# Retention's output in three float32r products, the norms' scaling on VectorE, and two tiles for a bias

## The chip, the cores and the metric

The kernel runs on one core of a Trainium2 chip, in one launch. The metric is device time in microseconds (us) of that core, from three runs of the kernel. An execution taken by the hardware profiler gives the span, which is the time from the first to the last instruction, and the busy time of each engine: TensorE (PE, with PEld for its weight loads), VectorE (DVE), ScalarE (ACT), GpSimd (POOL) and SyncE (SP), whose queue issues the DMAs.

## The reference

The reference is a stack of four layers on x of shape 8 x 1024 x 256, in float32, each of the form x + layer(layernorm(x)):

```python
x = x + _L0_attn_a_ref(_layernorm(x), ...)   # retention, 4 heads; itself returns its input + out
x = x + _L0_ffn_ref(_layernorm(x), ...)      # f
x = x + _L0_attn_b_ref(_layernorm(x), ...)   # softmax attention, 16 heads of 16, relative bias
x = x + _L0_ffn_ref(_layernorm(x), ...)      # g, the same weights as f
```

In the retention layer the input is normed once more with a weight and a bias (`ln_w`, `ln_b`), projected to q, k, v and a gate g, and after the heads it ends in

```python
o = o * lax.rsqrt((o ** 2).mean(-1, keepdims=True) + EPS) * g_norm_w
o = o * (g * jax.nn.sigmoid(g))
out = o.reshape(B, T, 2 * D) @ Wo        # (T x 512) @ (512 x 256) per batch
return x + out
```

The attention layer has scores q k / 4 plus a bias that depends on the distance of query and key alone (32 buckets), a softmax over 1024 keys, and projections with biases.

## The kernel before

**How it is written.** `layer_kernel` does not issue instructions itself. Each call on an engine (`act`, `dve`, `pool`, `sp`, `pe`) is recorded by `Plan.record` with an estimated cost (`Plan.estimate` for ACT, DVE and POOL, the `cost` argument in `mm` for PE) and a target time. Then `Plan.issue` plays all operations on five queues, picks for each engine the ready operation with the earliest target, and emits it (`emit`, line 609, which is why every row of the profile has this line). What results is a fixed order for each engine. `RULES` and `TURNS` steer the choice on PE: each stretch of 20 planned microseconds has one of 16 rules, one hexadecimal digit of `TURNS` each. On the chip every engine runs its list in that order and waits where data are late, so a change of any estimate, or of `TURNS`, moves instructions everywhere.

**The work.** The batches b = 0 to 7 go through retention, the first feed-forward (`ffn_front`), the projections of the attention (`project_b`), the attention itself, and `back` (its output and the second feed-forward). Targets let them overlap: while batch b is in its attention, batch b + 1 runs its retention.

- `retention(b)`: for four chunks of 256 tokens, `prepare` loads x and finds its mean and variance; `turn_chunk` computes the normed z (`normed`), scales x itself by s1 and m1 for the residual, transposes z on PE into `ntp`, and makes two float32r parts `nT[0]`, `nT[1]` of it, high and low, whose sum is the float32 value. For eight blocks of 128 tokens, `project` makes queries and keys (`qps`), values (`vps`) and gates (`gps`) by `mm3`: three float32r products of parts (low x high, high x low, high x high). `attend` leaves the gated heads in `gs`; `turn_gated` transposes them into `gtp` and copies them back into `gs`; `output` multiplies by `wo_a`, in plain float32, into `wps`, which is added to x.
- `normed` (lines 854 to 862) serves four norms: "a" in the retention, "f" and "g" in the feed-forwards, "b" ahead of the attention. Each is two ScalarE activations of 128 x 256 with a scale and a bias per partition.
- `project_b`: queries and keys by `mm3` into `qkp`; ScalarE adds the bias and writes `res` (the queries in reversed order), a cast makes the high part, and POOL (DVE in the first batch) the low part. Both go to `stk` in DRAM, from which `load_pair` reads them for a pair of heads.
- `maxima(b, j)`: for each pair of heads, scores p of 128 queries by 512 keys (`two`: two matmuls of 64 rows each, on two halves of the array); DVE finds the row maxima, from `jmax` with the near bias `hk1` added and from a plain reduction for the rest, into `pm`.
- `weigh(b, g)`: for four heads, scores s with keys on the partitions; ScalarE takes the exponential into `e2` (six tiles). Where a near bias must be added (`hank`, tag `hk2`, three tiles), ScalarE copies that part out, POOL adds the bias, and ScalarE takes the exponential. PE sums the weighed values in `acc`, four heads side by side in the array's columns.
- PSUM: one bank for `acc` and seven tiles of the tag "one" (`misc`), shared by everything else on PE.

**What the steps touch.** The norms' results feed the transposes (`ntp`, `ftp`, `btp`) on PE; p tiles come free when DVE has read them, s tiles when ScalarE has. DVE's list holds maxima, norms' statistics, token mixing (`xr`, `xk`) and retention's elementwise work one after the other; POOL's holds the additions `e<-e,hk`, small steps of the norms, and subtractions that make low parts. `swift(b == 0)` puts some work of the first batch on DVE in place of POOL. `const`, `tile2k`, `small` and `plan.tile` take SBUF tiles, where the last number is how many there are of a tag.

Of the kernel before, what the change touches and what calls it, by code (L numbers as in the profile page):

```python
# [10 lines left out]
F32 = mybir.dt.float32  # L11
# [68 lines left out]
    "00001700f08ff825e9a10f4bfe3f7f5b737f8bc37b237273e3f16482a6fe755707160591be52e6e5"  # L80
    "788ff00f76ff5fc03fdf6bfdd4ccf65b3b9c0cf84111"
# [230 lines left out]
class Plan:  # L312
# [15 lines left out]
    class Op:  # L328
        __slots__ = ("eng", "calls", "cost", "tail", "before", "after", "target", "mode", "news",
                     "wait", "ready", "done", "n", "tiles", "out", "group")  # L330
# [29 lines left out]
    def estimate(eng, method, n, views, kw):  # L360
# [4 lines left out]
        if eng == "DVE":  # L365
            if method == "reciprocal":
                return 0.1 + n / 160.0
            if method == "tensor_scalar":
                return 0.13 + n / 1920.0

            return 0.07 + n / 960.0 + 0.055 * (method == "scalar_tensor_tensor" and kw["scalar"])
# [7 lines left out]
    def record(self, eng, real, method, args, kw):  # L379
# [5 lines left out]
        if method in ("matmul", "transpose"):  # L385
            out, group = outs[0].t, kw.pop("group", None)
            op = self.last
            if op is None or op.group is not group or group is None and op.out[0] is not out:
                op = self.new(eng)
                op.out, op.cost, op.group = [], 0.0, group  # L390
                if args[1].dtype == F32R and args[1].shape[0] == P:
                    op.cost = 0.12
                self.last = op
                k, m = args[1].shape[0], 1
                for n in args[1].shape[1:]:
                    m *= n
                op.mode = ("rows" if k == 64 and m == P else "cols") if k == 64 or m == 64 else "all"
                if out.tag == "acc":
                    op.mode = "acc"
            if out not in op.out:  # L400
                op.out.append(out)
# [56 lines left out]
    def issue(self):  # L458
# [59 lines left out]
        while made < len(ops):  # L518
            progress = False
            for e in names:  # L520
                while free[e] <= now:
# [46 lines left out]
                    if e == "PE" and op.mode != mode:  # L568
                        took += SWITCH
# [43 lines left out]
def layer_kernel(ctx: ExitStack, tc: tile.TileContext, ap: dict, out: bass.AP):  # L613
# [26 lines left out]
    def mm(o, lhsT, rhs, start=True, stop=True, share=1.0, group=None):  # L640
        n = 1
        for d in rhs.shape[1:]:
            n *= d
        pe.matmul(o, lhsT, rhs, start=start, stop=stop, group=group,
                  cost=share * (0.005 + (4 if rhs.dtype == F32 else 1) * max(n, 64) / 2280.0))
# [37 lines left out]
    wo_a = const([P, RH, D], "wo_a")  # L683
# [39 lines left out]
    def next_ones():  # L723
# [3 lines left out]
        sp.dma_start(wo_a, ap["a_Wo"].rearrange("(h p) n -> p h n", p=P))  # L727
        sp.dma_start(gn, ap["a_gn"])

    def scale_out():  # L730

        dve.tensor_scalar(wo_a, wo_a, gn, 0.5, ALU.mult, ALU.mult)
# [121 lines left out]
    def normed(xc, mv, rs, name):  # L854
# [3 lines left out]
        for n in range(2):  # L858
            act.activation(
                z[:, n], xc[:, n], AF.Identity, scale=rs[:, n : n + 1], bias=nb[:, n : n + 1]  # L860
            )
# [13 lines left out]
    def retention(b):  # L875
# [20 lines left out]
        def turn_chunk(c):  # L896
# [3 lines left out]
            for n in range(2):  # L900
                act.activation(
                    t[:, n], t[:, n], AF.Identity, scale=s1[:, n : n + 1], bias=m1[:, n : n + 1]
                )
# [3 lines left out]
            for t in (nT[0], zT):  # L907
                for c in range(ND):
                    act.activation(
                        t[:, c], ps[:, c], AF.Identity,  # L910
                        scale=ln[:, 0, c : c + 1], bias=ln[:, 1, c : c + 1],
                    )
# [45 lines left out]
        def turn_gated(n):  # L958
# [4 lines left out]
            act.copy(gs, gtp)  # L963
            return gs

        def output(n, gT):
            wps = misc("wps")
            for h in range(RH):
                mm(wps[:, :D], gT[:, h * P : (h + 1) * P], wo_a[:, h, :], h == 0, h == RH - 1)
# [201 lines left out]
    def project_b(b):  # L1171

        for ch in range(NC):
# [10 lines left out]
            for s, w in ((0, "wq"), (1, "wk")):  # L1184
# [9 lines left out]
                res = plan.tile([P, 2, CT], F32, "res", "res", 1)  # L1194
                step = slice(None, None, -1) if s == 0 else slice(None)
                for blk in range(2):
                    bias = bqk[:, s, blk : blk + 1]
                    act.activation(res[:, blk, step], ps[:, blk], AF.Identity, bias=bias)
                act.copy(pt[0], res)
                swift(b == 0).tensor_tensor(pt[1], res, pt[0], ALU.subtract)  # L1200
# [33 lines left out]
    def two(ps, q, k, qc, kc, queries):  # L1234

        group = object()
        for hh in range(2):
            r = slice(hh * HROWS, (hh + 1) * HROWS)
            a, m = (k[r, kc], q[r, qc]) if not queries else (q[r, qc], k[r, kc])
            mm(ps[hh] if isinstance(ps, list) else ps[:, hh, :], a, m, share=0.5, group=group)  # L1240
# [69 lines left out]
    def weigh(b, g):  # L1310
# [140 lines left out]
```

## Time and profile before

| | |
|---|---|
| runs | 2562.29, 2563.42 and 2563.48 us; median 2563.42 |
| profiled execution | 2565.35 us; its span 2563.6 us |
| PE | 2477.1 us busy, 15814 matmul records |
| DVE, ACT, POOL | 2100.9, 2071.3 and 1591.6 us busy |
| granted TensorE clock | 0.992 of full speed |
| z, all four norms | 256 activations, 623 to 630 ns mean |
| wps, float32 | 512 matmul records, 127.4 us busy |

A float32 matmul shows as two records, a float32r matmul as one. The duration of a record is longer than the time to the next one's start, since instructions of one engine overlap a little; busy time counts overlap once. In a row of the profile, "out<-in" names the tiles, and "idle before" is the time that the engine stood still ahead of these instructions.

### The profile page before, as it was taken

How to read it: one execution, taken by the hardware profiler on the slowest of the kernel's cores; microseconds unless marked ns; L12 is line 12 of the kernel's file. 1: busy time of each engine (PE TensorE's matmuls, PEld its weight loads, DVE VectorE, ACT ScalarE, POOL GpSimd, SP SyncE). 2: the span in 40 equal slices, each digit the busy share in tenths (PEclk: the TensorE clock that was granted, in tenths of full speed). 3: DMA queues.
4: the chain of work that ended last, by engine and by line, in shares of the span. 5: the costliest groups of instructions: out<-in, count | busy, mean ns of one | idle time of the engine just before them, and what ended most of it. 6: DMA issues, size and time to landing. Idle time of an engine off the chain costs nothing.

```text
span 2563.6 us, 51515 instructions
## 1 busy us (share of the span) xinstructions
PE 2477.1 (97%) x15814; PEld 1462.6 (57%) x15814; DVE 2100.9 (82%) x6230; ACT 2071.3 (81%) x5334; POOL 1591.6 (62%) x2675
## 2 busy tenths in 40 slices
PE   5998999999999999999999999999999999999997
PEld 3886755555555556555655555555555555554555
DVE  6766988888898888888888888888888888887855
ACT  3564588898989988988889889888998888787783
POOL 3465675666666667766666676666666666665642
PEclk9999999999999999999999999999999999999999
DMA  7136132343424244433234343333243324444322
GB/s 174 42 104 150 55 92 64 92 120 99 111 74 114 78 97 119 123 82 95 71 101 110 98 109 97 89 103 89 81 115 97 101 76 132 120 114 109 92 65 67
DMA packets 252225, 251.18 MB, mean 98 GB/s; under 512 B 89042, under 2 KB 226180, under 8 KB 251924
## 3 DMA queue, kind: packets, MB, share of 16 engines
q1 hardware_dynamic: 251956, 247.89, 35.9%
q8 instruction: 132, 2.16, 0.4%
q14 instruction: 137, 1.12, 0.2%
HBM read 151.32 MB, written 98.59 MB: 97 GB/s over the span
## 4 chain that ended last, share of the span: by engine, by line
PE 78%; DVE 9%; ACT 4%; DMA 3%; POOL 3%; issue 2%; SPq 1%; POOLq 0%; DVEq 0%; ACTq 0%
PE acc L609 16%; PE p L609 10%; PE s L609 10%; PE wps L609 4%; PE yps L609 4%; PE kps L609 4%; PE rps L609 4%; PE gps L609 3%; PE qps L609 3%; DVE pm L609 3%; PE qkp L609 3%; PE vps L609 3%; PE ops L609 3%; ACT e L609 2%; PE bop L609 2%
## 5 line engine op out<-in xcount | busy, mean ns | idle before, releaser
L609 DVE TENSOR_REDUCE pm<-p 128x1 f32<-128x512 f32 (+2 forms) x2048 | 1057.7, 557 | 80.8 <-PE p L609 78.0
L609 ACT ACTIVATE e<-s 128x512 f32<-128x512 f32 (+2 forms) x2048 | 1010.6, 530 | 37.9 <-PE s L609 35.5
L609 POOL TENSOR_TENSOR e<-e,hk 128x512 f32<-128x512 f32 (+1 forms) x558 | 613.1, 1106 | 303.2 <-ACT e L609 296.5
L609 DVE CUSTOM_DVE_ANT_0 jmax<-p,hk 128x256 bf16<-128x256 f32 (+1 forms) x1152 | 427.1, 371 | 122.1 <-PE p L609 117.6
L609 PE MATMUL acc<-e,va 128*17 128x512 f32 x4096 | 524.5, 597 | 0.1
L609 PE MATMUL p<-k,q 64*128 64x512 f32 x2048 | 459.7, 438 | 10.7 <-DMA k<-stk 9.2
L609 ACT COPY e<-s 128x256 f32<-128x256 f32 (+1 forms) x1116 | 402.8, 361 | 83.3 <-PE s L609 80.3
L609 PE MATMUL s<-q,k 64*128 64x512 f32 x2048 | 453.2, 438 | 2.4 <-DVE pm L609 1.0
L609 ACT ACTIVATE e<-e 128x512 f32<-128x512 f32 (+1 forms) x576 | 336.8, 587 | 55.7 <-POOL e L609 52.9
L609 PEld LDWEIGHTS p<-k,q 64*128 64x128 f32 x2048 | 211.0, 185 | 248.2 <-ACT e L609 79.4
L609 PEld LDWEIGHTS s<-q,k 64*128 64x128 f32 x2048 | 205.2, 185 | 203.3 <-issue 63.0
L609 PEld LDWEIGHTS acc<-e,va 128*17 128x17 f32 x4096 | 79.7, 95 | 187.7 <-issue 162.1
L609 PE MATMUL rps<-W_r,xr 128*128 128x256 f32 x512 | 128.6, 393 | 12.8 <-DVE xr L609 10.6
L609 PE MATMUL yps<-W_v,xk 128*128 128x256 f32 x512 | 126.2, 389 | 4.7 <-DVE xk L609 3.4
L609 PE MATMUL wps<-wo_a,gs 128*128 128x256 f32 x512 | 127.4, 392 | 0.9 <-ACT gs L609 0.7
L609 PE MATMUL kps<-xk,W_k 128*128 128x256 f32 x512 | 125.7, 388 | 2.5 <-DVE xk L609 0.9
L609 PEld LDWEIGHTS rps<-W_r,xr 128*128 128x128 f32 x512 | 93.1, 192 | 44.3 <-issue 16.6
L609 PE MATMUL qps<-wqk,nT 128*128 128x512 f32 x384 | 109.4, 421 | 7.1 <-DVE nT L609 5.9
L609 PEld LDWEIGHTS yps<-W_v,xk 128*128 128x128 f32 x512 | 92.2, 190 | 32.1 <-issue 7.7
L609 PEld LDWEIGHTS kps<-xk,W_k 128*128 128x128 f32 x512 | 92.7, 190 | 30.5 <-issue 9.3
L609 PE MATMUL vps<-wv_a,nT 128*128 128x512 f32 x384 | 107.2, 415 | 2.4 <-DVE xc L609 1.8
L609 PEld LDWEIGHTS wps<-wo_a,gs 128*128 128x128 f32 x512 | 93.5, 192 | 25.6 <-ACT e L609 3.4
(182 smaller groups left out, 4135.5 us busy)
## 6 DMA issues: line engine op xcount, KB each, us to landing
stk<-qk SPq DMA_DIRECT2D x192, 256.0 KB
hk<-ud SPq DMA_DIRECT2D x128, 256.0 KB
q<-stk SPq DMA_DIRECT2D x128, 256.0 KB
k<-stk SPq DMA_DIRECT2D x128, 256.0 KB
od<-o SPq DMA_DIRECT2D x64, 256.0 KB
vd<-vst SPq DMA_DIRECT2D x64, 136.0 KB
va<-vd SPq DMA_DIRECT2D x32, 272.0 KB
xc<-in_x SPq DMA_DIRECT2D x32, 256.0 KB
```

Source lines behind the costliest of these rows:

```text
L609: getattr(real, method)(*[be(a) for a in args], **{k: be(a) for k, a in kw.items()})
```

## The change

- `wo_a` is kept as two float32r parts, made in `scale_out` from a load through the tiles `xo0` and `xo1`. `turn_gated` makes two parts of the transposed gated heads: a copy by ScalarE and a subtraction from PSUM by DVE, in the new tiles `gT0` and `gT1`. `output` uses `mm3`.
- `normed`, and the scaling of x by s1 and m1, become DVE `tensor_scalar` instructions with two scalars per partition.
- `turn_chunk` writes zT alone from PSUM; `nT[0]` becomes a DVE copy of zT.
- In `project_b` ScalarE writes the high part with the bias straight from PSUM, and DVE the low part, (ps + bias) - high; the tile `res` is gone.
- `hk2` has two tiles in place of three.
- The planner's costs are new (DVE's tensor_scalar and copies, matmuls, a later first matmul after a change of the array's shape), and so is `TURNS`.

```diff
 TURNS = (
-    "00001700f08ff825e9a10f4bfe3f7f5b737f8bc37b237273e3f16482a6fe755707160591be52e6e5"
-    "788ff00f76ff5fc03fdf6bfdd4ccf65b3b9c0cf84111"
+    "017e8737114e18fbf1fb389dfe783b3d618836f7fe7104348f3fbc1810a0770ba4998dde8e974dd8"
+    "7185e9e3764fd4f6e3f13024e98991f157bb75f111"
 )
...
-            if method == "tensor_scalar":
-                return 0.13 + n / 1920.0
+            if method in ("tensor_scalar", "tensor_copy") and all(v.t.space == "sbuf" for v in views):
+                return 0.07 + n / 1920.0 + 0.055 * kw["scalar"]
...
-                if args[1].dtype == F32R and args[1].shape[0] == P:
-                    op.cost = 0.12
...
+                op.late = (0.055 if method == "transpose" else 0.1) if op.mode == "all" else 0.0
...
-                        took += SWITCH
+                        took += SWITCH + op.late
...
-                  cost=share * (0.005 + (4 if rhs.dtype == F32 else 1) * max(n, 64) / 2280.0))
+                  cost=share * (0.004 + (4 if rhs.dtype == F32 else 1) * max(n, 64) / 2400.0))
...
-    wo_a = const([P, RH, D], "wo_a")
+    wo_a = [const([P, RH, D], f"wo_a{i}", F32R) for i in range(2)]
...
-        sp.dma_start(wo_a, ap["a_Wo"].rearrange("(h p) n -> p h n", p=P))
         sp.dma_start(gn, ap["a_gn"])
 
     def scale_out():
 
-        dve.tensor_scalar(wo_a, wo_a, gn, 0.5, ALU.mult, ALU.mult)
+        for i in range(2):
+            t = tile2k(f"xo{i}", 2).rearrange("p (h n) -> p h n", h=2)
+            h = slice(2 * i, 2 * i + 2)
+            sp.dma_start(t, ap["a_Wo"][2 * i * P : 2 * (i + 1) * P].rearrange("(h p) n -> p h n", p=P))
+            dve.tensor_scalar(t, t, gn, 0.5, ALU.mult, ALU.mult)
+            act.copy(wo_a[0][:, h], t)
+            dve.tensor_tensor(wo_a[1][:, h], t, wo_a[0][:, h], ALU.subtract)
...
         for n in range(2):
-            act.activation(
-                z[:, n], xc[:, n], AF.Identity, scale=rs[:, n : n + 1], bias=nb[:, n : n + 1]
-            )
+            dve.tensor_scalar(z[:, n], xc[:, n], rs[:, n : n + 1], nb[:, n : n + 1], ALU.mult, ALU.add)
...
             for n in range(2):
-                act.activation(
-                    t[:, n], t[:, n], AF.Identity, scale=s1[:, n : n + 1], bias=m1[:, n : n + 1]
-                )
+                dve.tensor_scalar(t[:, n], t[:, n], s1[:, n : n + 1], m1[:, n : n + 1], ALU.mult, ALU.add)
...
-            for t in (nT[0], zT):
-                for c in range(ND):
-                    act.activation(
-                        t[:, c], ps[:, c], AF.Identity,
-                        scale=ln[:, 0, c : c + 1], bias=ln[:, 1, c : c + 1],
-                    )
+            for c in range(ND):
+                act.activation(
+                    zT[:, c], ps[:, c], AF.Identity, scale=ln[:, 0, c : c + 1], bias=ln[:, 1, c : c + 1]
+                )
+            dve.tensor_copy(nT[0], zT)
...
-            act.copy(gs, gtp)
-            return gs
+            gT = [tile2k(f"gT{i}", 1, F32R) for i in range(2)]
+            act.copy(gT[0], gtp)
+            dve.tensor_tensor(gT[1], gtp, gT[0], ALU.subtract)
+            return gT
...
-                mm(wps[:, :D], gT[:, h * P : (h + 1) * P], wo_a[:, h, :], h == 0, h == RH - 1)
+                mm3(wps[:, :D], [t[:, h * P : (h + 1) * P] for t in gT], [t[:, h, :] for t in wo_a],
+                    h == 0, h == RH - 1)
...
-                res = plan.tile([P, 2, CT], F32, "res", "res", 1)
...
-                    act.activation(res[:, blk, step], ps[:, blk], AF.Identity, bias=bias)
-                act.copy(pt[0], res)
-                swift(b == 0).tensor_tensor(pt[1], res, pt[0], ALU.subtract)
+                    hi, lo = (t[:, blk, step] for t in pt)
+                    act.activation(hi, ps[:, blk], AF.Identity, bias=bias)
+                    dve.scalar_tensor_tensor(lo, ps[:, blk], bias, hi, ALU.add, ALU.subtract)
...
-            mm(ps[hh] if isinstance(ps, list) else ps[:, hh, :], a, m, share=0.5, group=group)
+            mm(ps[hh] if isinstance(ps, list) else ps[:, hh, :], a, m, share=0.525, group=group)
...
-        hank = [near_bias(2 * g + i, "hk2", 3) for i in range(2)]
+        hank = [near_bias(2 * g + i, "hk2", 2) for i in range(2)]
...
-                       es[j // 2][:, j % 2, :], n == 0, n == NT - 1, share=0.243)
+                       es[j // 2][:, j % 2, :], n == 0, n == NT - 1, share=0.2535)
```

More of the change, by code (lines that the diff above doesn't have):

```diff
@@ L329 @@
         __slots__ = ("eng", "calls", "cost", "tail", "before", "after", "target", "mode", "news",
-                     "wait", "ready", "done", "n", "tiles", "out", "group")
+                     "wait", "ready", "done", "n", "tiles", "out", "group", "late")
     def __init__(self, ctx, tc):
```

## The prediction

> **What bounds the kernel now.** I read the page's busy line and slices first, then the stretches, PE's matmul rows and its order of work in time, the waits, and last the rows of the operations that move.
>
> ```profile
> PE 2477.1 (97%) x15814; PEld 1462.6 (57%) x15814; DVE 2100.9 (82%) x6230; ACT 2071.3 (81%) x5334; POOL 1591.6 (62%) x2675
> ...
> DVE  6766988888898888888888888888888888887855
> ```
>
> ```profile
> 640.00:960.00 320.00, 318.25 (x2079) 175.46 (x2078) 281.81 (x855) 282.64 (x746) 206.59 (x321) 1.00 0.36 94
> ...
> sum 1600.00, PE 1588.01 PEld 904.70 DVE 1370.86 ACT 1400.54 POOL 1049.20; mean PE 317.60 PEld 180.94 DVE 274.17 ACT 280.11 POOL 209.84
> ```
>
> The stretches (columns: length, then busy time of PE, PEld, DVE, ACT, POOL) say it most clearly: from 640 to 2240 us PE is busy 1588.0 of 1600 us. The whole middle is TensorE's own work, and only 12 us there are idle. ACT stands at 87.5%, DVE at 85.7%. PE's work is therefore counted first, and DVE's load is the thing to watch.
>
> ```profile
> 1210.05 1.99 PE L609 MATMUL wps<-wo_a,gs 128*128 128x256 f32 x8
> 1211.98 0.50 PE L609 MATMUL p<-k,q 64*128 64x512 f32 x2
> 1212.31 0.40 PE L609 MATMUL s<-q,k 64*128 64x512 f32 x2
> 1212.54 0.40 PE L609 MATMUL p<-k,q 64*128 64x512 f32 x2
> ```
>
> ```profile
> 1233.61 1.66 PE L609 MATMUL qkp<-hT,bwq 128*128 128x256 f32 x12
> 1235.11 1.53 PE L609 MATMUL bvp<-bwv,hT 128*128 128x256 f32 x12
> 1236.57 0.50 PE L609 MATMUL s<-q,k 64*128 64x512 f32 x2
> ```
>
> Matmul records overlap, so the cost of a group is from its start to the next start: retention's output in plain float32 (four matmuls, eight records) costs 1.93 us, and twelve float32r products of the same shape cost 1.46 to 1.50. A pair of p or s costs 0.23, or 0.33 when it borders on a group that uses the array in another shape: a change of shape is worth 0.1 us.
>
> **The change, part by part.**
>
> *Retention's output.* Four float32 matmuls become twelve float32r ones per block of 128 tokens, 64 blocks. Most wps groups stand between p and s pairs and cost 1.92. The nearest row for the new one is bvp (turned tokens as weights, 256 moving columns): 1.575 between other shapes as the median of its groups in the trace, qkp 1.61. Gain 64 x 0.35 = 22 us (20 by qkp's price, 24 if the loads hide better).
>
> *The order.* The planner's costs and its table of turns are new, so the whole order is. Counted in both programs, runs of matmuls of one array shape rise from 1937 to 1961. At 0.1 to 0.2 us each that is 2 to 5 us. Pricing each group of the new order by the median of its kind and neighbours in the old trace gives 10 us more for everything but wps. I take +8, ends 2 and 10. PE's own work: -14 us.
>
> *ScalarE.* It loses 320 norm activations (256 z, 64 xc, 0.49 us apart when back to back), 64 nT activations (0.45) and 64 casts of res (0.52): 157 + 29 + 33 = 219 us. This can only help by PE's idle time in the middle, 12 us in 1600.
>
> *VectorE* gets:
> - 64 subtractions gT from PSUM, 512 wide: the like row (gs, ta, vs) starts its next 0.60 later: 38 us.
> - 128 scalar_tensor_tensor from PSUM, 256 wide, with a scalar per partition: the xr/xk row below runs at 0.40 without a hold-up: 51 us, less the 8 subtractions of 0.6 us of the first batch that go: 46.
> - 320 tensor_scalar with two scalars, 256 wide, SBUF to SBUF, and 32 copies of 512: no row has them. The setup's tensor_scalar of 16x1024 takes 734 ns and follows itself after 0.66. A quarter of its columns scales that to 0.17 with no fixed part; a full-rate operation of 256 (xk) costs 0.40. Taking a fixed 0.1 plus a quarter of the rest, and a little for the second scalar, 0.28: 90 us (54 to 128). The copies 0.34: 11 us.
>
> Sum 185 us. scale_out's two loads, four more operations and PE's wait at the start happen once: 0 to 3 us, cover DVE's setup work; I take 0.
>
> *The hold-up between DVE and POOL.*
>
> ```profile
> L609 DVE SCALAR_TENSOR_TENSOR xr<-xk,mu,zT x128: 451/480/1531, 81.8 to 2551.6; 128x256 f32<-128x256 f32 x128
> L609 DVE SCALAR_TENSOR_TENSOR xk<-xk,mu,zT x128: 386/476/1508, 82.6 to 2552.4; 128x256 f32<-128x256 f32 x128
> ```
>
> The columns are shortest/median/longest ns. DVE operations that read two tiles of SBUF take 480 ns as a rule and up to 1531: at 2108.52 two of them take 2.93 us in place of 0.88, while POOL's additions of 1.27 us run beside them. The means, 621 and 609 ns, put the average hold-up at 0.14 us. PSUM reads such as gs<-gs,gps never show it. If each of the 352 new SBUF-to-SBUF operations pays as much, DVE gets 49 us more; ends 0 and 100 (twice that, as they follow POOL's small products and POOL is busy 62%).
>
> The Trainium skill (SBUF — State Buffer, "Who interferes with whom") speaks against this part: tensor_scalar and copies in a two-port mode and any GpSimd operation shut each other out for a whole instruction. It fits the long records above; no row here shows it for a full-width tensor_scalar. By the rule alone an estimate is 0.34 us each (62% of the time POOL is busy, with half an addition of 1.1 us left on average), 120 us in all; DVE would stand at 2406 us and the sum would be that of the first rival.
>
> So DVE goes from 2101 to about 2335 us. The middle holds 1600 of the some 2400 us over which the eight batches run, two thirds of the new 234 us: 1371 + 156 of 1590 us, 96% in place of 85.7%. Today ACT runs at 87.5% beside a PE that never waits long, so a high load alone does not stop PE. Seven PSUM buffers are shared by p and s:
>
> ```profile
> PEld p L609 <- ACT e L609: 79.4, 135, 0.9
> ...
> PEld p L609 <- DVE pm L609: 55.2, 74, 0.9
> ...
> PEld s L609 <- DVE pm L609: 43.1, 82, 0.9
> ...
> PEld s L609 <- ACT e L609: 29.4, 51, 0.9
> ```
>
> These waits (total, times, longest) are for buffers, short, and split evenly: 109 us for ACT, 98 for DVE. ACT's will shrink, DVE's grow. I let them cancel (+0; ends -12, all of the middle's idle time gone, and +60, which is DVE's share growing by 60%).
>
> *POOL* loses 56 subtractions of 1.3 us: 73 us, off the path. *hk2 with two tiles* instead of three: the next group's bias is loaded only when the last near tile of this one is done. A load took 2.75 and 3.20 us where the chain shows it, 32 groups: at most 115 us if bare. Six e buffers let PE, and ACT's copies, run on, and p pairs fill in; POOL, first to wait, is idle a third of the time. 0 taken. Its issue sits in SP's queue ahead of q, k and stk loads, which are issued a pair of heads early.
>
> *The end.* Four chunks of the last block run nearly alone; two norm operations at 1.09 us per pair become 0.6. Four times 0.5: -2 us.
>
> **Sum.** 2563.6 - 22 + 8 - 2 = 2547.6 us of span; 1.75 us lie around it (profiled run 2565.35). That execution is 1.9 above the median, so 2547.4; I say 2548.
>
> **The rivals.**
> 1. *DVE becomes the bound; slower.* DVE's idle time in the middle, 229 of 1600 us, must take two thirds of 185 us, 123, and of the hold-ups. With 100 us of those DVE is 98% busy (1371 + 123 + 67 of 1590); then every 1.3 us hold-up reaches PE, because there is nothing to catch up with. PE losing 2 to 3% of 1900 us is 38 to 57, less 16: 2585 to 2604. It decides once the hold-up passes some 0.2 us per operation, 70 us in all. For it: long xk records, two in a row. Against: DVE waits 196 us for p (jmax 117.6, pm 78.0 among the waits), so it runs ahead now.
> 2. *Gain and stall cancel.* Stalls of 10 to 20 us eat the 16: 2559 to 2568.
> 3. *The float32r groups cost as much as before.* If weight loads (twelve instead of eight records, 188 ns each) bound them, the 22 us go and +8 of order stays: 2569. Against it stands bvp at 1.46.
>
> **How the numbers follow.** Faster as forecast 0.50 (own range 2530 to 2556); rival 1 0.34; rival 2 0.12; rival 3 0.04. The times of this kernel tell 0.2%, 5 us, from no change. The forecast lies below that bound almost wholly; rival 2 gives 0.03 to faster and the rest to same. Faster 0.53, same 0.10, slower 0.37. Low end: -24 + 2 - 12 - 2 and a DVE at its cheapest, with 10 us for what the new order may hide: 2517. High end: rival 1's middle, 2596.
>
> **What would show it.** Twelve wps records per group and 1.57 from start to start; DVE near 2335 busy, tensor_scalar groups near 0.3 us with a tail above 1 us; ACT near 1850; POOL near 1520; PE busy over 99% of the middle. Wrong if PE's idle time or its p and s spacing grows beside waits for "DVE pm", or if z's mean passes 0.5 us.

## The result, and the profile after

The changed kernel takes **2646.9 us** (median of four runs, 2639.5 to 2651.2), the kernel before beside it 2562.9 us (2562.0 to 2563.5). The ratio is 1.032 (95% interval 1.031 to 1.034): 84 us **slower**, where 15 us faster was forecast. The profiled execution took 2645.8 us, with a span of 2644.1, 80.5 more than before.

The busy line and VectorE's slices of the page:

```profile
PE 2506.6 (95%) x16070; PEld 1476.0 (56%) x16070; DVE 2334.2 (88%) x6769; ACT 1881.2 (71%) x4888; POOL 1529.5 (58%) x2619
...
DVE  6988998999999899998988999899998899888964
```

The loads came out as forecast: VectorE 2334 us (forecast 2335), ScalarE 1881 (1850), POOL 1530 (1520). What did not follow is the time. The stretches (length, then busy time of PE, PEld, DVE, ACT and POOL):

```profile
640.00:960.00 320.00, 312.93 (x2093) 177.08 (x2091) 296.28 (x881) 254.30 (x673) 193.84 (x326) 1.00 0.34 93
...
sum 1600.00, PE 1554.85 PEld 877.37 DVE 1464.01 ACT 1251.61 POOL 967.55; mean PE 310.97 PEld 175.47 DVE 292.80 ACT 250.32 POOL 193.51
```

PE now has 45 us of idle time in the middle 1600, where it had 12, although VectorE is 91.5% busy there and not full, and ScalarE has fallen to 78%. A busy PE is not a fast one either: its busy time rose by 29.5 us, although the output's groups need less, so the group prices are needed. PE's order in time:

```profile
1259.88 1.69 PE L608 MATMUL wps<-wo_a,gT 128*128 128x256 f32 x12
1261.50 0.50 PE L608 MATMUL p<-k,q 64*128 64x512 f32 x2
1261.84 0.40 PE L608 MATMUL s<-q,k 64*128 64x512 f32 x2
1262.07 0.40 PE L608 MATMUL p<-k,q 64*128 64x512 f32 x2
```

The new output group costs 1.62 from its start to the next start, against 1.93: the gain on PE came. To see all of PE I took for every group of matmuls in a trace the time from its start to the next group's start, and the median of that over groups into the same tile, with as many records and the same array shapes ahead of them and behind them, in the same trace. The sum of the medians is an estimate of what PE's order costs without stalls; what is left over is stalls. Before: 2426 + 113 us. After: 2427 + 195 us. The split depends on how finely the groups are sorted. Other sortings put the rise of the stalls between 63 and 109 us, and PE's own work between 28 us lower and 19 higher. In all of them the stalls are most of the 82 us. The output's groups alone fell from 120 to 102 us.

The rows of two of the operations that moved to VectorE (shortest, median and longest ns):

```profile
L608 DVE TENSOR_SCALAR z<-xc,f_y,f_nb x64: 392/407/1407, 81.8 to 2180.1; 128x256 f32<-128x256 f32 x64
...
L608 DVE TENSOR_SCALAR z<-xo,g_y,g_nb x64: 380/409/1462, 645.9 to 2622.2; 128x256 f32<-128x256 f32 x64
```

And those of the two that were held up before:

```profile
L608 DVE SCALAR_TENSOR_TENSOR xr<-xk,mu,zT x128: 380/477/1570, 85.6 to 2632.0; 128x256 f32<-128x256 f32 x128
L608 DVE SCALAR_TENSOR_TENSOR xk<-xk,mu,zT x128: 462/475/1551, 86.8 to 2632.8; 128x256 f32<-128x256 f32 x128
```

A z of 256 columns records 408 ns as a rule and up to 1462; the mean over all 256 of them is 574 ns, so a hold-up of 0.17 us on average. The waits (total, times, longest), three rows of before first, then those of the changed kernel:

```profile
DVE jmax L609 <- PE p L609: 117.6, 167, 2.2
...
DVE pm L609 <- PE p L609: 78.0, 103, 8.9
...
ACT e L609 <- POOL e L609: 52.9, 73, 5.4
```

```profile
ACT e L608 <- PE s L608: 190.6, 277, 4.6
...
ACT e L608 <- POOL e L608: 117.2, 141, 4.8
PEld p L608 <- ACT e L608: 89.3, 141, 2.9
...
POOL e L608 <- DMA hk<-ud: 66.6, 29, 4.1
...
PEld s L608 <- DVE pm L608: 60.3, 112, 0.9
DVE jmax L608 <- PE p L608: 59.9, 88, 4.0
...
PEld p L608 <- DVE pm L608: 53.8, 83, 1.1
DVE pm L608 <- PE p L608: 53.6, 74, 5.2
...
PEld s L608 <- ACT e L608: 28.9, 49, 0.9
```

Two things stand out. ScalarE lost 190 us of work, and yet PE waits no less for it (118 us in place of 109): ScalarE now waits itself, 117 us for POOL's additions (53 before), and POOL waits 67 us for the near bias to land (2 before). And VectorE waits for p only 113 us in place of 196: it runs ahead of PE much less often.

The main thing is in neither pair of rows alone. Summed over the whole trace, all waits of PE's matmuls and weight loads that end with VectorE grow from 238 to 342 us, and those that end with ScalarE from 247 to 270. Weight loads wait beside running matmuls, so these sums are not lost time one for one.

### The profile page after: what moved, and what is told of

Its sections match the earlier page's. It is cut to its first block, busy times and chain, and to the rows that moved or that the text cites. A ratio compares the mean times of both kernels' runs of the same rounds, so it can differ in the third digit from the quotient of the medians.

```text
span 2644.1 us, 51948 instructions
## 1 busy us (share of the span) xinstructions
PE 2506.6 (95%) x16070; PEld 1476.0 (56%) x16070; DVE 2334.2 (88%) x6769; ACT 1881.2 (71%) x4888; POOL 1529.5 (58%) x2619
## 4 chain that ended last, share of the span: by engine, by line
PE 63%; DVE 19%; DMA 9%; POOL 3%; ACT 3%; issue 2%; SPq 1%; POOLq 0%; DVEq 0%; ACTq 0%
PE acc L608 13%; PE p L608 9%; PE s L608 8%; DVE pm L608 7%; DMA hk<-ud 3%; PE rps L608 3%; PE yps L608 3%; PE kps L608 3%; PE ops L608 3%; PE qps L608 3%; PE vps L608 3%; PE wps L608 3%; PE gps L608 3%; PE qkp L608 3%; DVE jmax L608 2%
## 5 line engine op out<-in xcount | busy, mean ns | idle before, releaser
L608 ACT ACTIVATE e<-s 128x512 f32<-128x512 f32 (+2 forms) x2048 | 996.4, 519 | 73.3 <-PE s L608 70.6
L608 PE MATMUL acc<-e,va 128*17 128x512 f32 x4096 | 536.3, 600 | 16.2 <-ACT e L608 14.3
L608 PE MATMUL p<-k,q 64*128 64x512 f32 x2048 | 472.6, 440 | 13.1 <-ACT e L608 4.8
L608 PE MATMUL s<-q,k 64*128 64x512 f32 x2048 | 471.3, 443 | 10.4 <-DMA q<-md 4.1
L608 ACT COPY e<-s 128x256 f32<-128x256 f32 (+1 forms) x1116 | 390.1, 350 | 123.1 <-PE s L608 120.0
L608 ACT ACTIVATE e<-e 128x512 f32<-128x512 f32 (+1 forms) x576 | 329.9, 574 | 122.9 <-POOL e L608 117.2
L608 PEld LDWEIGHTS s<-q,k 64*128 64x128 f32 x2048 | 211.6, 185 | 239.6 <-issue 66.0
L608 POOL TENSOR_TENSOR ao_y<-ao_a,mhalf 128x4 f32<-128x4 f32 x64 | 67.0, 1047 | 81.6 <-DVE ao_a L608 81.1
L608 PE MATMUL wps<-wo_a,gT 128*128 128x256 f32 x768 | 109.6, 293 | 1.9 <-DVE gT L608 1.9
L608 PEld LDWEIGHTS wps<-wo_a,gT 128*128 128x128 f32 x768 | 97.2, 192 | 19.2 <-DVE pm L608 4.3
```

Source lines behind the costliest of these rows:

```text
L608: getattr(real, method)(*[be(a) for a in args], **{k: be(a) for k, a in kw.items()})
```

## The experiments

Three theories were set against each other. (1) The two tiles for the near bias: its loads come late, POOL waits, ScalarE and PE behind it. (2) VectorE's load: its new work, its hold-ups behind POOL, or both. (3) The order: the planner's costs are not the chip's, and the new order fits the plan and not the chip. Where a kernel of the study keeps the exact order of another, the planner's order is fixed first and single instructions are then exchanged or added in their places.

The chips differ by a few us, so below each time stands its excess over the kernel before as a share of 2563 us, from the ratio measured on the same chip.

### The order planned again

One edit each, and the planner makes a new order from it: the changed kernel with three bias tiles, the kernel before with two, and the kernel before with nothing but the other table of turns.

```diff
-        hank = [near_bias(2 * g + i, "hk2", 2) for i in range(2)]
+        hank = [near_bias(2 * g + i, "hk2", 3) for i in range(2)]
```

(here the squares of the retention share the tile `at`, for room)

> The changed kernel with three tiles for the near bias of the weighed heads again (the squares of retention share the tile of its masked scores, which makes the room). Theory 1, the two bias tiles: the loads come too late, POOL waits 66.6 us for them, and the exponentials and acc behind it; with three tiles 60 to 85 us come back: 2562 to 2590 us. Theory 2, VectorE's load and its hold-ups by POOL: no difference beyond 10 us, 2637 to 2657. Theory 3, the new order as such (planned with costs that are off): a new order again, 2630 to 2660.

Measured: 2683.6 us, ratio 1.047 (1.043 to 1.052), 121 us over before and 37 over the changed kernel, and outside all three ranges. The added room did not help: the planner made another order for it, and that one is slower.

```diff
-        hank = [near_bias(2 * g + i, "hk2", 3) for i in range(2)]
+        hank = [near_bias(2 * g + i, "hk2", 2) for i in range(2)]
```

> The kernel before with two tiles for that bias and nothing else. Theory 1: 50 to 85 us slower, 2613 to 2648. Theory 2: within 10 us of 2563. Theory 3: some 10 to 40 us slower from a new order alone, 2573 to 2603, without a wait of POOL for the bias of more than 20 us.

Measured: 2715.7 us, ratio 1.060 (1.053 to 1.067), +153 us, outside all three ranges too. POOL waits 57.0 us for the near bias there, so most of the 153 can't be that wait.

```diff
 TURNS = (
-    "00001700f08ff825e9a10f4bfe3f7f5b737f8bc37b237273e3f16482a6fe755707160591be52e6e5"
-    "788ff00f76ff5fc03fdf6bfdd4ccf65b3b9c0cf84111"
+    "017e8737114e18fbf1fb389dfe783b3d618836f7fe7104348f3fbc1810a0770ba4998dde8e974dd8"
+    "7185e9e3764fd4f6e3f13024e98991f157bb75f111"
 )
```

> The kernel before with the changed kernel's table of turns: the same work in another order. Theories 1 and 2: within 15 us of 2563. Theory 3: 2590 to 2640, since an order that was not made for this kernel costs what the change cost.

Measured: 2661.0 us, ratio 1.038 (1.034 to 1.043), +98 us, with not one instruction more or less, and above theory 3's range. By the group prices 27 us of it are PE's own (2453 in place of 2426) and 74 are stalls (187 in place of 113). What follows: a table of turns that was chosen for another program cost this one some 100 us. Runs in which the order is planned again without a new table say nothing about the part that was edited. From here on the order was held fixed.

### The changed kernel's order, single parts taken back

**The bias loads.** A third tile, and each load issued right behind the one before it; no other instruction moves (the squares of the retention lie in a tile that is free just then, for room).

```diff
+        for k, (v, op) in enumerate(biases):
+            v.t.slot = "hk2", k % 3
...
+        follow = {loads[k - 1]: loads[k] for k in range(2, len(loads))}
...
+            if op in follow:
...
+                res.append((follow[op], news[follow[op]]))
```

> The changed kernel with every engine's list as it was, but a third tile for the near bias and each of its loads standing in SyncE's list right behind the load before it (the squares of retention lie in tiles that are free just then, which makes the room). Theory 1, late bias loads: POOL's 66.6 us of waiting for them go, and 30 to 60 us of the time: 2587 to 2617. Theories 2 (VectorE's load) and 3 (an order planned with wrong costs): within 10 us of 2647.

Measured: 2634.1 us, ratio 1.028 (1.026 to 1.031), +73 us, between the two ranges. POOL no longer waits for the bias, and ScalarE's wait for POOL falls from 117 to 81 us, but only 10 us (0.4%) come back. The late loads are real and small.

**The norms.** The 320 tensor_scalar go back to ScalarE, in VectorE's places.

```diff
-            dve.tensor_scalar(z[:, n], xc[:, n], rs[:, n : n + 1], nb[:, n : n + 1], ALU.mult, ALU.add)
+            op = dve.tensor_scalar(z[:, n], xc[:, n], rs[:, n : n + 1], nb[:, n : n + 1], ALU.mult, ALU.add)
+            on_act(op, z[:, n], xc[:, n], rs[:, n : n + 1], nb[:, n : n + 1])
...
+    def on_act(op, out, src, scale, bias):
+        op.calls[0] = (nc.scalar, "activation", (out, src, AF.Identity), dict(scale=scale, bias=bias))
```

> The changed kernel in exactly its order, but the 320 scalings of the norms issued on ScalarE at the places where VectorE had them. VectorE loses some 155 us with the hold-ups, ScalarE gains 157. Theory 1: within 10 us of 2647. Theory 2: most of what was lost comes back, 2580 to 2610. Theory 3: within 15 us of 2647.

Measured: 2651.0 us, ratio 1.034 (1.031 to 1.038), +88 us: no gain, though VectorE is down to 2200 us. Both edits together, the early bias loads and the norms on ScalarE:

> The same with the scalings of the norms issued on ScalarE in VectorE's places. If VectorE's load was hidden behind the late loads, it shows now: 20 to 40 us below the run with early loads. Theories 1 and 3: within 10 us of that run.

Measured: 2636.7 us, ratio 1.029 (1.027 to 1.032), +75 us. And with the norms' scaling left out altogether, the transposes reading what was to be scaled:

```diff
+            op.calls = [(None, "", (), {})]
...
+                x = unscaled[id(src)][1][:, i, c * P : (c + 1) * P]
+                plan.last.calls[-1] = real, method, (args[0], x, args[2]), kw
```

> The changed kernel in its order without the 320 scalings of the norms on any engine: the transposes read unscaled x, and x is not scaled for the residual (this part of the computation is left out). VectorE loses some 150 us, nothing is added elsewhere, and POOL is no longer held up by them. Theory 2 (VectorE's work in the way): 2560 to 2605 us. Theory 3 (the order is made for costs that the chip does not have, z among many): 2630 to 2650.

Measured: 2615.9 us, ratio 1.021 (1.019 to 1.023), +54 us, between the two ranges. Leaving 134 us of VectorE's work out returns 31 us; moving it to ScalarE returns nothing. In the run with the norms on ScalarE, PE's waits that end with VectorE fall from 342 to 278 us, and those that end with ScalarE rise from 270 to 364: the wait changes its engine. Read alone, these runs spoke against theory 2, and for a loss that is spread over the order. The next two sets speak against that reading.

### Before's order, single parts put in

**The norms on VectorE**, in ScalarE's places:

```diff
-            act.activation(
+            op = act.activation(
                 z[:, n], xc[:, n], AF.Identity, scale=rs[:, n : n + 1], bias=nb[:, n : n + 1]
             )
+            op.calls[0] = (nc.vector, "tensor_scalar", (z[:, n], xc[:, n], rs[:, n : n + 1], nb[:, n : n + 1], ALU.mult, ALU.add), {})
```

> The kernel before with its own lists, but the 320 scalings of the norms issued on VectorE at the places where ScalarE had them: VectorE gets 105 us of work and some 50 us of hold-ups (2101 to about 2256 us busy), ScalarE loses 157. Theory 2: 20 to 50 us slower, 2583 to 2613. Theory 3: 2558 to 2578, since the order, which was good, is the same.

Measured: 2631.2 us, ratio 1.027 (1.025 to 1.030), **+70 us**, from one part alone, with ScalarE relieved of 136 us. That is above the range of theory 2, and far above that of theory 3.

**The output in three products**, with the subtraction right behind ScalarE's copy, and the same without the subtraction (the low part replaced by the high one):

```diff
-            act.copy(gs, gtp)
+            op = act.copy(gs, gtp)
...
+            op.calls = [
+                (nc.scalar, "copy", (gT[0], gtp), {}),
+                (nc.vector, "tensor_tensor", (gT[1], gtp, gT[0], ALU.subtract), {}),
+            ]
...
+            op.calls = [
+                (nc.tensor, "matmul", (wps[:, :D], gT[i][:, h * P : (h + 1) * P], wo[j][:, h, :]),
+                 dict(start=h == 0 and m == 0, stop=h == RH - 1 and m == 2))
+                for h in range(RH) for m, (i, j) in enumerate(((1, 0), (0, 1), (0, 0)))
+            ]
```

> The kernel before with its own lists, but retention's output by three float32r products: twelve matmuls where four stood, VectorE's subtraction for the low part right behind ScalarE's copy, the new tiles in memory that is free just then. All theories: TensorE's work falls by 64 times 0.30 to 0.35 us. Theory 3 (the order decides, and this one stays): 2538 to 2548. Theory 2: VectorE's 38 us more eat half of it or more, 2548 to 2566.

```diff
-            gT.append(plan.guest([P, HALF], F32R, "gT1", [op], tags=TWO))
+            gT.append(gT[0])
...
-                (nc.vector, "tensor_tensor", (gT[1], gtp, gT[0], ALU.subtract), {}),
```

> The kernel before in its order with the twelve float32r matmuls, but without VectorE's subtraction: the low part of the gated heads is left out, and its product reads the high part again. TensorE's work is that of the run with three products. If VectorE's 38 us, met at places that the plan had not kept free, took the gain away (theory 2 and its weaker form, lateness in a tight order): 2538 to 2550 us. If the matmuls or their weight loads did: 2570 to 2582.

Measured: 2580.4 us with it, ratio 1.007 (1.006 to 1.009), **+19 us**; 2551.3 without, ratio 0.995 (0.994 to 0.997), **-12 us**. The first is above both of its ranges. So PE's float32r groups do gain, 12 us of the 20 by their measured price (64 times 1.92 less 1.61), and 64 subtractions, which add 36.5 us to VectorE's busy time (2136.2 against 2099.7), cost 31. In the groups of the run with the subtraction (count, busy, mean ns, idle before):

```profile
L650 DVE TENSOR_TENSOR gT<-gtp,gT 128x512 fp32r<-128x512 f32 x64 | 44.3, 692 | 40.7 <-ACT gT L650 39.5 <-POOL f_t L650 1.0
```

VectorE stands idle 40.7 us ahead of them, waiting for ScalarE's copy with its list behind it. That looked like the cause, and so the subtraction was put one or two of VectorE's instructions later (not behind the next use of the PSUM buffer that it reads), and the products that need it last:

```diff
+            banks = [t.slot for t in news if t.space == "psum"]
+            for h in [h for h in held if h[1] == 0 or ends[h[0]] is op or lows_bank[h[0]] in banks]:
...
+                out.append((h[0], []))
...
+            if op in lows:
+                held.append([lows[op], 2])
...
-                for h in range(RH) for m, (i, j) in enumerate(((1, 0), (0, 1), (0, 0)))
+                for m, (i, j) in enumerate(((0, 1), (0, 0), (1, 0))) for h in range(RH)
```

> Before's order with the output by three float32r products, as in the run that took 2580.4 us, but VectorE's subtraction of the low part stands one or two of VectorE's instructions later in its list (never behind the next use of the PSUM buffer it reads), and the four products that need the low part come last of the twelve. In that run VectorE stood idle 40.7 us ahead of its 64 subtractions, 39.5 of it waiting for ScalarE's copy, with its whole list behind. Theory 2 (VectorE's load): the same 44 us of work are there, so the time stays at 2574 to 2584 us, 24 to 34 above the run without the subtraction (2551.3). Theory 3 (the order: where the new work stands in the list, not how much it is): most of those 40 us of waiting go, and with it most of the loss, 2554 to 2566 us, at or below the kernel before (2563).

Measured: 2581.6 us, ratio 1.009 (1.008 to 1.010), +23 us: no better, and in theory 2's range. The groups of VectorE and PE:

```profile
L651 PE MATMUL p<-k,q 64*128 64x512 f32 x2048 | 468.1, 439 | 19.1 <-DMA k<-stk 8.8 <-DVE gT L651 8.3 <-DVE tb L651 0.6
...
L651 DVE TENSOR_TENSOR gT<-gtp,gT 128x512 fp32r<-128x512 f32 x64 | 43.7, 682 | 1.6 <-ACT gT L651 1.6
```

The 40 us of waiting on VectorE are gone (1.6), and PE waits instead: p's matmuls wait 8.3 us for "DVE gT", the buffer that the later subtraction still reads (1.7 in the run before). The wait moved and the cost stayed. Then the low part was made without VectorE: ScalarE makes the high part from its copy in SBUF, and POOL subtracts.

```diff
+                (nc.scalar, "copy", (gs, gtp), {}),
+                (nc.scalar, "copy", (gT[0], gs), {}),
+                (nc.gpsimd, "tensor_tensor", (gT[1], gs, gT[0], ALU.subtract), {}),
```

> Before's order with the output by three float32r products, the low part made without VectorE: ScalarE copies the turned heads out of PSUM as before, makes the high part from that copy in SBUF (64 more instructions, about 0.5 us each, 33 us), and POOL subtracts (64 of about 1.3 us, 83 us); the products with the low part come last. Theory 2 (VectorE's load): VectorE has no new work, ScalarE and POOL have room in the profile (81% and 62% busy), so the time is that of the run without the subtraction plus little: 2551 to 2560 us, a gain on the kernel before. Theory 3 (the order): work put into any list that was timed without it costs about what it is wherever others wait behind it; ScalarE's 33 us show as 10 to 30 us: 2562 to 2582 us.

Measured: 2628.2 us, ratio 1.027 (1.026 to 1.028), +69 us, by far the worst of the three, on the engines with the most room, and above both ranges. The waits:

```profile
ACT e L650 <- POOL e L650: 95.2, 106, 5.3
PEld p L650 <- ACT e L650: 94.1, 165, 2.1
...
POOL gT L650 <- ACT gT L650: 66.2, 50, 4.5
```

POOL waits 66 us for the new copy with the additions of the weighed heads behind it, ScalarE waits 95 us for POOL (53 before), and PE 94 for ScalarE (79). Here the idle share of an engine (ScalarE's 19%, POOL's 38%) was no measure of the room in its list. Only this one placing of the new work was tried.

### The order chosen anew

The same work as in the changed kernel, but the planner has the costs of the traces, and the table of turns is chosen for them:

```diff
+            if method == "tensor_scalar" and n == 256:
+                return 0.45
+            if method == "scalar_tensor_tensor" and views[0].t.tag[:2] in ("xr", "xk") and n == 256 and views[1].t.space == "sbuf":
+                return 0.5
...
+                if args[1].dtype == F32R and args[1].shape[0] == P:
+                    op.cost = 0.083
...
-                op.cost, op.tail = 0.4, 2.0 + size / 100000.0
+                op.cost, op.tail = 0.4, 3.0 + size / 80000.0
```

> The changed kernel's work and tiles, unchanged; the planner is given costs from the traces (tensor_scalar of 256 columns with its mean hold-up 0.45 us in place of 0.26, xr and xk from two SBUF tiles 0.5, a float32r pass of 128 rows 0.083 in place of 0.107, a load's landing one us later), and the table of turns is chosen anew under these costs, so that the order fits the work. Busy times stay as in the changed kernel (VectorE 2334 us). Theory 3 (the order was planned with wrong costs): 2600 to 2632 us, 15 to 45 below the changed kernel (2646.9). Theory 2 (VectorE's load and the hold-ups, whatever the order): 2638 to 2660 us.

With the same costs, the norms planned on ScalarE and three bias tiles (the squares of the retention lie in a tile that is free just then, for room):

```diff
-            dve.tensor_scalar(z[:, n], xc[:, n], rs[:, n : n + 1], nb[:, n : n + 1], ALU.mult, ALU.add)
+            act.activation(z[:, n], xc[:, n], AF.Identity, scale=rs[:, n : n + 1], bias=nb[:, n : n + 1])
...
-        hank = [near_bias(2 * g + i, "hk2", 2) for i in range(2)]
+        hank = [near_bias(2 * g + i, "hk2", 3) for i in range(2)]
```

> The same corrected costs and an order chosen for them, but the norms' scaling planned on ScalarE, and three tiles for the near bias; the output by three float32r products, the cast of the first part and the attention's queries and keys stay as in the changed kernel. VectorE is some 2190 us busy, ScalarE 2030. Theory 2 (VectorE's load): the 134 us and the hold-ups are gone, 2565 to 2595 us, clearly below the run above. Theory 3 (the order): the order fits the work in both, so this one is below the run above only by what the planner sees, some 25 us. If both gains add it reaches the kernel before (2563); I expect 2575 to 2600.

Measured: 2646.2 us with the norms on VectorE, ratio 1.032 (1.030 to 1.034); 2590.6 with the norms on ScalarE and three bias tiles, ratio 1.011 (1.009 to 1.013). The first run's busy line and the sum of its stretches, then the second's:

```profile
PE 2518.8 (95%) x16070; PEld 1474.2 (56%) x16070; DVE 2339.3 (88%) x6769; ACT 1875.1 (71%) x4888; POOL 1530.1 (58%) x2619
```

```profile
sum 1600.00, PE 1554.79 PEld 887.03 DVE 1454.21 ACT 1230.84 POOL 973.69; mean PE 310.96 PEld 177.41 DVE 290.84 ACT 246.17 POOL 194.74
```

```profile
PE 2486.3 (96%) x16070; PEld 1470.1 (57%) x16070; DVE 2198.9 (85%) x6449; ACT 2013.3 (78%) x5208; POOL 1525.3 (59%) x2619
```

```profile
sum 1600.00, PE 1567.86 PEld 894.32 DVE 1402.15 ACT 1330.96 POOL 982.34; mean PE 313.57 PEld 178.86 DVE 280.43 ACT 266.19 POOL 196.47
```

A wholly different order of the same work lands on the same time, in theory 2's range, and has the same 45 us of idle PE in the middle. So nothing here shows that the changed kernel's order was a bad one for its work, though two orders don't show that no better one exists. Taking the norms off VectorE, with an order chosen for that and a third bias tile, is worth 56 us (theory 3 had given some 25). The tile has a part in it that was not measured alone: POOL waits 29.5 us for the near bias in the first run, and not at all in the second. The second is still slower than the kernel before, and no version of the change that ran beat it, but for the one that leaves the low part out.

### Load, hold-ups, or waiting for the norms

The last set adds work that nobody needs to the kernel before, in its own order, at the 320 places where ScalarE scales a norm; ScalarE keeps that. Once it is a maximum over 256 columns of a spare tile, once the norms' own instruction on that tile:

```diff
+            op.calls.append((nc.vector, "tensor_reduce", (spares[1][:, :1], spares[0], AX.X, ALU.max), {}))
```

```diff
+            op.calls.append((nc.vector, "tensor_scalar", (spares[0], spares[0], spares[1][:, :1], spares[1][:, 1:], ALU.mult, ALU.add), {}))
```

> The kernel before in its own order, nothing moved; at each of the 320 places where ScalarE scales a norm, VectorE gets one instruction more that nobody needs and that waits for nothing: a maximum over 256 columns of a spare tile (about 0.33 us start to next, one SBUF tile read, so no hold-up behind POOL). VectorE about 2200 us busy, ScalarE unchanged. If VectorE's load as such costs the time (theory 2a), 2600 to 2635 us, much of the 69 us that the norms on VectorE cost in this order. If the hold-ups behind POOL cost it (2b), or the wait of others for the norms' results (2c), the added work vanishes in VectorE's idle time (18% of the span): 2566 to 2585 us.

> The same 320 places, but the added instruction that nobody needs is the norms' own kind: a tensor_scalar with two scalars per partition over 256 columns of the spare tile, which POOL holds up (0.33 us plus some 0.16). VectorE about 2235 us busy. Theory 2a: 10 to 25 us above the run with the maximum (load and hold-ups cost alike, by their length). Theory 2b: 35 us or more above it, 2610 to 2640. Theory 2c (others wait for the norms' results): near the run with the maximum and far below the 2631 us of the norms on VectorE, 2570 to 2595.

The share of the engines in the chain of work that ended last, before, and then the rows (shortest, median and longest ns), that share and the busy line with the maximum and with the tensor_scalar:

```profile
PE 78%; DVE 9%; ACT 4%; DMA 3%; POOL 3%; issue 2%; SPq 1%; POOLq 0%; DVEq 0%; ACTq 0%
```

```profile
L649 DVE TENSOR_REDUCE spare<-spare x320: 360/411/422, 19.0 to 2580.7; 128x1 f32<-128x256 f32 x160
```

```profile
PE 72%; DVE 16%; ACT 3%; DMA 3%; POOL 3%; issue 2%; SPq 1%; POOLq 0%; DVEq 0%; ACTq 0%
```

```profile
PE 2504.0 (96%) x15814; PEld 1472.6 (57%) x15814; DVE 2197.1 (84%) x6552; ACT 2076.4 (80%) x5334; POOL 1591.5 (61%) x2675
```

```profile
L649 DVE TENSOR_SCALAR spare<-spare x320: 315/409/1521, 18.8 to 2611.7; 128x256 f32<-128x256 f32 x160
```

```profile
PE 65%; DVE 22%; ACT 4%; POOL 3%; DMA 3%; issue 3%; SPq 0%; POOLq 0%; DVEq 0%; ACTq 0%
```

```profile
PE 2516.9 (96%) x15814; PEld 1476.2 (56%) x15814; DVE 2241.6 (85%) x6552; ACT 2078.6 (79%) x5334; POOL 1599.1 (61%) x2675
```

Measured: 2601.8 us with the maximum, ratio 1.016 (1.014 to 1.018), **+42 us**; 2639.2 with the tensor_scalar, ratio 1.031 (1.029 to 1.033), **+80 us**. Both instructions record about 410 ns when nothing holds them. The maximum never takes longer than 422. Of the 320 tensor_scalar 80 took over 600 ns, up to 1521; the excess over the median sums to 48 us. So 96 us of plain work on VectorE, 18% idle, which nobody waits for, cost 42 (0.43 us for each), and 48 us of hold-ups cost another 38 (0.8 us for each). POOL is hardly held up in turn: it is busy 8 us longer, and ScalarE's wait for it stays at 55 us. The norms' own results add nothing that shows: moved for real they cost 70, less than the 80. But ScalarE is relieved at the same time, and no run separates the two. In the chain VectorE's share goes from 9% before to 16, 22 and, in the changed kernel, 19%.

Last, both moved parts at once in before's order (the exchange of the norms and the three products, as in the diffs above):

> The kernel before in its own order with two parts of the change at once: the output by three float32r products (alone +18 us) and the norms' scaling on VectorE (alone +69). hk2 keeps three tiles, and the attention's queries and keys and the first part's cast stay as before. If the parts simply add (theory 2, VectorE's load): 2640 to 2665 us, the whole loss of the changed kernel without its order or its two tiles. Theory 3 (the changed kernel's order makes a good part of its loss): 2600 to 2630.

Measured: 2650.3 us, ratio 1.035 (1.034 to 1.037), **+90 us**. The single parts give 70 + 19 = 89. They add, and in size they are the whole loss: the changed kernel, with an order of its own, stands at +84. The waits fit: those of PE that end with VectorE sum to 264 us with the maximum, 299 with the tensor_scalar and 344 here, against 238 before and 342 in the changed kernel.

## Why the prediction was wrong

**The step that failed** is the one on PE's waits for buffers: "ACT's will shrink, DVE's grow. I let them cancel (+0; ends -12 [...] and +60)". The stalls rose by 82 us (63 to 109, as the groups are sorted). ScalarE's part did not shrink: its two buffer waits went from 109 to 118 us, since ScalarE waits for POOL and PE where it had work before. VectorE's part grew, but hardly in the rows that the prediction looked at: the two buffer waits that end with "DVE pm" stand at 114 us where they stood at 98, while all of PE's waits that end with VectorE grew by 104. The upper end, "DVE's share growing by 60%", scaled a row that measures the wrong thing.

The reason given, "a high load alone does not stop PE", since ScalarE ran at 87.5% beside a PE that never waits long, took idle time for slack. The maximum that nobody needs shows it directly: 82% busy, VectorE charged 0.43 us for every us of new work. A likely reading is that the order is timed for each engine at its load, and that seven PSUM buffers let none run far ahead, so that a later VectorE reaches PE wherever the order has no room left. No run changed the number of buffers, so this reading is not shown.

Summed with the prices of the runs: norms +70 (load 42 and hold-ups 38, less 10 that ScalarE's relief may have given back), subtraction +31, PE's products -12, together +89 against +90 for the two parts in before's order and +84 for the whole change. That leaves -6 for the rest. The bias loads are 10 of it, so the low part, the casts and the order of the changed kernel come to about -16 together; they were not measured each on its own.

**The other steps.**
- *Retention's output*: nearly right. 1.62 for 1.575 forecast, so 19 us of PE's work for the forecast 22. In before's order 12 us reach the time. Rival 3 falls.
- *The order*: +8 forecast; the group prices give about +19 for everything but wps, other sortings -10 to +37, so this term stays open. An order that doesn't fit its program is dear (+98).
- *VectorE's durations*: right in the sum (2335 against 2334). The tensor_scalar alone was low: it starts its next 0.32 us later, not 0.28.
- *The hold-ups*: right in size, 0.15 to 0.17 us against 0.14 each. The row had also shown two in a row; that they reach PE was in rival 1 alone. The sign "z's mean passes 0.5 us" came true, at 574 ns.
- *hk2 at no cost*: the cover that was named (six e buffers, POOL's idle third) is thinner than thought. POOL waits 67 us, and 10 reach the end. (32 times 3.20 us is 102 us, not 115; on the changed kernel's chain these loads took up to 8.6 us.)
- *ScalarE's -219 and the end's -2*: ScalarE lost 190, and it helped little, as said. The end's 2 us were not measured alone; in the last 160 us PE is busy 136 us where it was 143, so no gain shows there.

**The rivals.** Rival 1 had the right engine and the right sign, at 0.34, and its price fell short: 2585 to 2604. It let VectorE's load bite only when it is 98% busy and hold-ups pass 0.2 us. VectorE is 91.5% busy in the middle (96% were forecast), the hold-ups are 0.16, and it bites all the same. With the added maximum it bites at 84% of the span, without hold-ups of the new work: no such threshold shows. The range ended at about the middle of that rival, 2596, and so left out the result. The profile held a warning that the prediction did not weigh: VectorE's waiting for p, 196 us, which it took as proof of a lead, was less than the 234 us of new work.

The page of the Trainium skill that was weighed (SBUF — State Buffer, "Who interferes with whom") is where the prediction's estimate of 120 us for the hold-ups came from. The rows give 50 us for the 320 instructions in the changed kernel (the excess over the median) and 48 for the added ones. Its other statement, that a tensor_reduce never contends with GpSimd while a tensor_scalar from SBUF to SBUF can, agrees with the two added instructions: 422 ns at the longest against 1521.

## What to carry to other kernels

In this program, whose engines run fixed lists beside a TensorE that is 97% busy, the idle share of another engine was not room. Plain new work on VectorE cost 0.43 of its length, the subtractions between ScalarE and PE 0.85 (31 of 36.5 us), hold-ups 0.8. Where a program is built like this, set such a sum against TensorE's gain first, and don't count on relief: ScalarE's 136 us, taken off it, gave back some 10 us at most. Test a part by putting it alone into the old order. Taking the norms out of the new order showed 31 us or nothing for a part worth 70, and letting a planner make a new order for a bias tile more or less measured 37 and 153 us of something else.

## What the runs showed of the hardware

- A tensor_scalar of 128 x 256 float32 with two scalars per partition, SBUF to SBUF, records 408 ns and, when nothing holds it, starts its next 0.32 us later. A quarter of them (80 of the 320 added ones) is held up, to 1.5 us at most, and each of these 80 ends 0.15 us after the end of an instruction on POOL. A tensor_reduce over the same 256 columns records 411 ns, starts its next 0.33 us later and is never held up (320 of 320): the tensor_scalar is hardly quicker.
- Operations of VectorE that read PSUM (the subtraction gT at 683 ns, the low part of queries and keys at 476 ns) show no hold-up in any run.
- In before's order VectorE's time had two prices: 0.43 us of run time per us for 96 us of even, short work, and 0.8 per us for 48 us that came in 80 lumps of up to 1.1 us.
